# First ternary product of a four-layer kernel: two float32r parts in place of four-pass float32

## The chip, the cores and the metric

The kernel runs on one core of one Trainium2 chip. The metric is the device time of one execution in microseconds. A core has TensorE (PE; its weight loads are listed apart as PEld), VectorE (DVE), ScalarE (ACT), GpSimd (POOL) and SyncE (SP, which here only issues DMAs). Each engine works through its own queue of instructions in order; semaphores hold an instruction back until what it reads or overwrites is ready.

## The reference

Four layers with a residual and a layernorm after each, on x of 8 x 512 x 256 float32:

```python
x = L0_attn_x
x = _layernorm(x + _L0_attn_ref(x, ...))   # retention, 16 heads of 16, group norm
x = _layernorm(x + _L0_ffn_ref(x, ...))    # ternary feed-forward, below
x = _layernorm(x + _L1_attn_ref(x, ...))   # attention across heads within a token
x = _layernorm(x + _L1_ffn_ref(x, ...))    # 8 experts, top 2 of each token, 160 slots
```

The change lies in the second:

```python
def _absmean_core(W):
    gamma = jnp.mean(jnp.abs(W)) + EPS
    Ws = W / gamma
    return jnp.sign(Ws) * jnp.minimum(jnp.round(jnp.abs(Ws)), 1.0), gamma

h = jnp.einsum('btd,hd->bth', x, absmean(W_fc))      # 256 -> 1024: the product that changes
h = jax.nn.gelu(h, approximate=False)
h = layernorm(h, ln_w, ln_b)
return jnp.einsum('bth,dh->btd', h, absmean(W_proj)) # 1024 -> 256
```

The weights of both products are -1, 0 or 1 after `absmean`.

## The kernel before, in words

One batch b is 512 tokens: four chunks of 128 rows, 256 columns. Each batch runs through six stages, written as Python generators:

- a1: transpose x to xT (256 on partitions), products q, k, v (L859, L883), then four chunks of retention: scores `sc` (L907), masked by VectorE, ScalarE and POOL, products into `r_ps` (L927 to L940), the running state (L949).
- a2: group norm, back-transpose (L1038), residual, layernorm. Its result x1 stays in SBUF.
- b: transpose x1 to x1T through `transposed` (L334), which puts four 128x128 transposes into one PSUM bank and copies the bank out with ScalarE, for each of the two halves k of the 256 inputs. Then for each of eight blocks f of 128 hidden units two matmuls of 128x512 into `fc_ps` (L1063), gelu on ScalarE into hT, a square on ScalarE, and a sum of the squares on POOL. Then four products `pr_ps` (L1092, eight matmuls of 128x257 each), with the statistics of the inner layernorm folded into the last step.
- bn: layernorm, plus the scale of the next RMS norm.
- c1: transpose to x2T, project four chunks (L1172, L1178), elu, VectorE transposes, head scores `hs` (L1231), masks, values `at_ps` (L1246).
- c2: a long normalizing part on VectorE, transpose to aT, two products with a gelu between (L1314, L1325), layernorm, transpose to xoT, router product (L1348).

Before them come p(0) (`prepare_ffn`: thresholds, ternary weights, their transposes into fcT and prT, bias sums) and p(1) (`prepare_l1`: the weights of c1 and c2). After the layers each of two groups of four batches is routed, its rows gathered, and 16 expert products run (L1455, L1484), with `finish` writing the output.

The order of instructions is not written by hand. `interleave` keeps the streams in a list, each with its stages in order; it always resumes the stage that can go on first by the plan's clock, and at equal times the one that stands first in the list. A stage says how long its matmuls take with `pe(cost)`, and `op(engine, cost, t, ...)` puts an operation into the first free spell of an engine from time t on. These costs are numbers in the code. They set the order in which each engine's queue is filled; the chip then runs the queues.

Buffers are rings with tags. A stage begins only when its `takes` are free. Tag "T" has three buffers (`TB = 3`, L150) of 128 x 2 x 512 float32 and holds xT (a1), x1T (b), x2T (c1), aT and xoT (c2, through `hold`). PSUM has eight banks of 128x512 float32, also handed out by the plan. The list of streams at L1557 runs: expert weights, x, c2, bn, c1, gather, dispatch, routing, a2, a1, p, b, combine, expert out, expert in, finish. So b ranks last among the stages of the layers.

The lines that matter for the change: `fcT` at L611, its copies at L675, stage b from L1052 to L1076, and the streams of a1, p and b at L1588 to L1599.

Of the kernel before, what the change touches and what calls it, by code (L numbers as in the profile page):

```python
# [10 lines left out]

F32 = mybir.dt.float32
I32 = mybir.dt.int32
AF = mybir.ActivationFunctionType
ALU = mybir.AluOpType
# [4 lines left out]
P = 128  # L20
# [60 lines left out]
def tile_layers(ctx: ExitStack, tc: tile.TileContext, ins, out, at):  # L81
# [82 lines left out]
    def give(tag, t, n=1):  # L164
        Plan.free[tag] += [t] * n
# [8 lines left out]
    def op(engine, cost, t, fn, *args, use=None, drop=None, bank=None, **kw):  # L174


        if engine in (GELU, EXP):
            cost += 0.0 if engine == Plan.loaded else TABLE
            engine, Plan.loaded = ACT, engine
        users = [engine]  # L180
        if engine in (DVS, POOL):
            users.append("port")
        engine = users[0] = {DVS: DVE, POOLD: POOL}.get(engine, engine)
        t = t + HOP
        if use is not None:
            t = max(t, take(use) + HOP)
        if engine != SP:
            length = max(cost - OVERLAP[engine], 0.05)
            found = False
            while not found:  # L190
                found = True
                for user in users:
                    for a, b in Plan.busy[user]:
                        if t + length <= a:
                            break
                        if b > t:
                            t, found = b, False
            for user in users:
                bisect.insort(Plan.busy[user], (t, t + length))
                while Plan.busy[user][0][1] < Plan.t - 30.0:  # L200
                    Plan.busy[user].pop(0)
        Plan.count += 1
        heapq.heappush(Plan.events, (t, Plan.count, lambda: fn(*args, **kw)))  # L203
        t += cost
        if drop is not None:
            give(drop, t)
        if bank is not None:
            release(bank, t)
        return t
# [5 lines left out]
    def pe(cost):  # L215

        Plan.now = Plan.t = max(Plan.now, Plan.t) + cost
        return Plan.now + PE_OUT

    def bank(name):  # L220
        i = Plan.banks.index(min(Plan.banks))
        assert Plan.banks[i] < HELD, name
        ps = psum.tile([P, 512], F32, tag=f"bank{i}", bufs=1, name=name)
        Plan.bank_of[id(ps)] = ps, i
        Plan.banks[i] = HELD
        return ps
# [4 lines left out]
    def need(t, n=1):  # L231

        while True:
            r = max(t + HOP_PE, sorted(Plan.banks)[n - 1] + HOP if n else 0.0)
            yield "pe", r if r < HELD else Plan.t + 0.5
            if not n or sorted(Plan.banks)[n - 1] <= Plan.t + 1e-6:
                return
# [90 lines left out]
    def transposed(dst, src, t, cost=0.5):  # L328

        for k in range(NK):  # L330
            yield from need(t)
            ps = bank("tp")
            for c in range(NC):
                T.transpose(ps[:, c * P : (c + 1) * P], src[:, c, k * P : (k + 1) * P], ident)  # L334
            done = op(ACT, 0.59, pe(cost), A.copy, dst[:, k, :], ps, bank=ps)
        return done
# [214 lines left out]
    with ExitStack() as stages:  # L551
# [56 lines left out]
        op(DVS, 1.0, 15.5, prepare_past)  # L608
        op(DVS, 0.85, 40.0, prepare_gn)

        fcT = fb.tile([P, NK, FF], F32, name="fcT")  # L611


        prT = fb.tile([P, NF, D + 1], F32, name="prT")
# [436 lines left out]

        def stage_b(b):  # L1052
            x1 = x1s.pop(b)
            x1T = wk.tile([P, NK, S], F32, tag="T", bufs=TB, name=f"x1T_{b}")
            turned = yield from transposed(x1T, x1, 0.0)

            hT = fb.tile([P, NF, S], F32, tag="big", bufs=1, name=f"fT_{b}")
            sq = fb.tile([P, S], F32, tag="fsq", bufs=1, name=f"fsq_{b}")
            for f in range(NF):
                yield from need(turned)  # L1060
                ps = bank("fc_ps")
                for k in range(NK):
                    T.matmul(  # L1063
                        ps, fcT[:, k, f * P : (f + 1) * P], x1T[:, k, :],
                        start=(k == 0), stop=(k == NK - 1),
                    )
                inner_ = op(GELU, 0.6, pe(1.73), A.activation, hT[:, f, :], ps, AF.Gelu, bank=ps)
                if f == 0:
                    squared = op(ACT, 0.62, inner_, A.activation, sq, hT[:, f, :], AF.Square)
                else:  # L1070
                    sf = wk.tile([P, S], F32, tag="ex", bufs=EX, name=f"fsf_{b}_{f}")
                    e = op(ACT, 0.63, inner_, A.activation, sf, hT[:, f, :], AF.Square, use="ex")
                    squared = op(
                        POOL, 1.29, max(e, squared), GP.tensor_tensor, sq, sq, sf, ALU.add, drop="ex"
                    )
            give("T", Plan.now)  # L1076
            x1b = x1
            based = op(
                POOL, 2.36, Plan.now, GP.tensor_tensor, x1b, x1, bc(prbias, 1, NC), ALU.add
            )  # L1080
            st = wk.tile([P, 3, NC], F32, tag="f_st", bufs=2, name=f"f_st_{b}")
            z = x1b
            ss = wk.tile([P, NC], F32, tag="f_ss", bufs=2, name=f"f_ss_{b}")
            accs, ends = [], []
            for c in range(NC):
                if c == 1:
                    yield from need(squared, n=2)
                else:
                    yield from need(inner_ - 0.5)
                acc = bank("pr_ps")  # L1090
                for f in range(NF):
                    T.matmul(  # L1092
                        acc[:, : D + 1], hT[:, f, c * P : (c + 1) * P], prT[:, f, :],
                        start=(f == 0), stop=(f == NF - 1),
                    )
                accs.append(acc)
                if c == 1:
                    ps = bank("ss_ps")
                    for i in range(NC):
                        T.matmul(  # L1100
                            ps[:, i : i + 1], sq[:, i * P : (i + 1) * P], ones[:, :1],
                            start=True, stop=True,
                        )
                t = op(
                    DVE, 0.15, pe(4.29 if c == 1 else 3.58), V.tensor_copy,
                    st[:, 0, c : c + 1], acc[:, D : D + 1],
                )
                if c % 2 == 0:
                    continue
                if c == 1:  # L1110
                    op(
                        DVE, 0.16, t, V.tensor_scalar, ss, ps[:, :NC], 1.0 / FF, LN_EPS, ALU.mult,
                        ALU.add, bank=ps,
                    )
                pair = slice(c - 1, c + 1)
                mu, var, rs = (st[:, i, pair] for i in range(3))

                def spread(pair=pair, mu=mu, var=var, rs=rs):

                    nc.vector.tensor_tensor(rs, mu, mu, ALU.mult)  # L1120
                    nc.vector.tensor_tensor(var, ss[:, pair], rs, ALU.subtract)
                    nc.vector.tensor_scalar(var, var, LN_EPS, None, ALU.max)

                t = op(DVS, 0.5, t, spread)
                t = op(
                    POOL, 0.7, t, GP.tensor_tensor, rs, var, mhalf.to_broadcast([P, 2]), ALU.pow
                )
                for c2 in (c - 1, c):
                    ends.append(op(
                        DVE, 0.48, max(t, based), V.scalar_tensor_tensor,  # L1130
                        z[:, c2, :], accs[c2][:, :D], st[:, 2, c2 : c2 + 1], x1b[:, c2, :],
                        ALU.mult, ALU.add, bank=accs[c2],
                    ))
            zs[b] = z, ends
            yield later(Plan.t)
            return Plan.t
# [415 lines left out]
        def after(*keys):  # L1552
            return [k for k in keys if k[1] >= 0 and (k[0] != "p" or k[1] < 2)]
# [32 lines left out]
            [(("a2", b), after(("a1", b)), {}, stage_a2(b)) for b in range(B)]  # L1586
            + [(("o", 0), [], {}, open_experts(0))],
            [  # L1588
                (("a1", b), after(("x", b), ("b", b - 3), ("p", b - 1)), {"aq": 3, "T": 1}, stage_a1(b))
                for b in range(B)  # L1590
            ],
            [
                (("p", 0), [], {"b8": 2}, prepare_ffn()),
                (("p", 1), [], {"m4": 1}, prepare_l1()),
            ],
            [
                (("b", b), after(("a2", b), ("p", 0), ("c1", b - 2)), {"T": 1}, stage_b(b))
                for b in range(B)
            ]  # L1599
            + [(("o", 1), [], {}, open_experts(1))],  # L1600
# [50 lines left out]
```

## Time and profile before

| what | us |
|---|---|
| median of 3 runs (lowest, highest) | 969.6 (968.71, 969.89) |
| the profiled execution, device time | 969.52 |
| its span, first to last instruction | 967.7 |
| TensorE busy | 905.1 |
| VectorE busy | 593.3 |
| ScalarE busy | 459.4 |
| POOL busy | 391.4 |

The span begins with the loading of x and the weights. p(0) ends near 53 us, b(0)'s first block begins at 70 us, and b(7)'s last `pr_ps` ends near 730 us. The experts follow, with the last stages of the layers in between, and `finish` ends the run. The mean granted clock of TensorE was 0.976 of full speed.

In the page, a row of part 5 gives the line, engine, operation, output and inputs, shapes and count, then the group's busy time in us, the mean time of one record in ns, and the idle time of the engine before the group with what ended most of it. L203 is the line in `op` through which all operations of the vector engines go, so for these the tile's name tells the place. Matmul records overlap, so the mean time of a record is longer than its share of the engine. A timeline row gives start, length, engine, line, operation, tiles, count, and in brackets the idle time before it with its releaser. The chain of waits, listed in order of time, gives start, length, engine, tile, line and count.

### The profile page before, as it was taken

How to read it: one execution, taken by the hardware profiler on the slowest of the kernel's cores; microseconds unless marked ns; L12 is line 12 of the kernel's file. 1: busy time of each engine (PE TensorE's matmuls, PEld its weight loads, DVE VectorE, ACT ScalarE, POOL GpSimd, SP SyncE). 2: the span in 40 equal slices, each digit the busy share in tenths (PEclk: the TensorE clock that was granted, in tenths of full speed). 3: DMA queues.
4: the chain of work that ended last, by engine and by line, in shares of the span. 5: the costliest groups of instructions: out<-in, count | busy, mean ns of one | idle time of the engine just before them, and what ended most of it. 6: DMA issues, size and time to landing. Idle time of an engine off the chain costs nothing.

```text
span 967.7 us, 18426 instructions
## 1 busy us (share of the span) xinstructions
PE 905.1 (94%) x7516; PEld 670.7 (69%) x7516; DVE 593.3 (61%) x1469; ACT 459.4 (47%) x868; POOL 391.4 (40%) x395
## 2 busy tenths in 40 slices
PE   7889999999999998999999999999999999999970
PEld 4766766676667665766776567667567798999960
DVE  2943447676766678457767878667756773513223
ACT  2345357347533755178515552763854544222213
POOL 3335434543452345344343453353554233254331
PEclk9999999999999999999999999999999999999985
DMA  7020000001001000100001000105203445429835
GB/s 226 10 88 2 1 1 2 1 23 44 2 1 66 1 2 1 66 2 2 1 22 45 1 2 1 45 2 180 66 1 105 140 146 173 110 53 344 272 64 179
DMA packets 49652, 60.34 MB, mean 62 GB/s; under 512 B 5536, under 2 KB 44960, under 8 KB 49568
## 3 DMA queue, kind: packets, MB, share of 16 engines
q1 hardware_dynamic: 45600, 53.92, 16.4%
q0 software_dynamic: 3968, 5.25, 3.0%
q8 instruction: 59, 0.97, 0.4%
q14 instruction: 25, 0.20, 0.1%
HBM read 43.43 MB, written 15.73 MB: 61 GB/s over the span
## 4 chain that ended last, share of the span: by engine, by line
PE 73%; DVE 15%; ACT 4%; POOL 3%; issue 3%; DMA 2%; POOLq 0%; ACTq 0%; SPq 0%; DVEq 0%; another core or an unknown queue 0%
PE fc_ps L1063 10%; PE pr_ps L1092 7%; PE wo_ps L1484 7%; PE wi_ps L1455 6%; PE qk_ps L1172 5%; PE qk_ps L859 5%; PE hs L1231 3%; PE at_ps L1246 3%; PE tp L334 3%; PE w_ps L1314 3%; DVE a L203 2%; PE r_ps L940 2%; PE v_ps L1178 2%; PE w_ps L1325 2%; PE sc L907 2%
## 5 line engine op out<-in xcount | busy, mean ns | idle before, releaser
L1092 PE MATMUL pr_ps<-prT,fT 128*128 128x257 f32 x512 | 118.4, 385 | 3.0 <-ACT aT L203 2.8
L1063 PE MATMUL fc_ps<-x1T,fcT 128*128 128x512 f32 x256 | 118.7, 601 | 1.4 <-ACT x1T L203 1.4
L1092 PEld LDWEIGHTS pr_ps<-prT,fT 128*128 128x128 f32 x512 | 96.1, 191 | 19.2 <-ACT aT L203 3.0
L203 POOL TENSOR_TENSOR fsq<-fsq,fsf 128x512 f32<-128x512 f32 x56 | 71.8, 1281 | 65.4 <-ACT fsf L203 65.0
L1063 PEld LDWEIGHTS fc_ps<-x1T,fcT 128*128 128x128 f32 x256 | 45.7, 190 | 47.7 <-issue 40.7
L1455 PE MATMUL wi_ps<-xsT,wi 128*128 128x160 f32 x512 | 74.9, 301 | 0.0
L1484 PE MATMUL wo_ps<-e_hT,wo 128*128 128x160 f32 x512 | 74.3, 300 | 0.0
L1484 PEld LDWEIGHTS wo_ps<-e_hT,wo 128*128 128x128 f32 x512 | 70.9, 190 | 1.5 <-issue 1.3
L1455 PEld LDWEIGHTS wi_ps<-xsT,wi 128*128 128x128 f32 x512 | 70.6, 190 | 0.7 <-ACT xsT L203 0.4
L203 DVE TENSOR_TENSOR hm<-hs,cst 128x512 f32<-128x512 f32 x96 | 59.8, 675 | 16.8 <-PE hs L1231 15.7
L203 POOL DMA_INDIRECT y_d<-eo,srci x24 | 37.5, 1560 | 80.3 <-ACT eo L203 26.5
L203 DVE TENSOR_TENSOR scm<-sc,cst 128x512 f32<-128x512 f32 x96 | 60.4, 679 | 14.3 <-PE sc L907 14.2
L203 POOL TENSOR_TENSOR ln_rs<-ln_rs,mhalf 128x4 f32<-128x4 f32 x32 | 34.3, 1073 | 81.1 <-DVE ln_rs L203 79.5
L203 ACT ACTIVATE e_hT<-wi_ps 128x480 f32<-128x480 f32 (+1 forms) x48 | 24.9, 526 | 86.6 <-PE wi_ps L1455 86.6
L203 POOL TENSOR_TENSOR scm<-scm,cst 128x512 f32<-128x512 f32 x32 | 41.6, 1300 | 50.3 <-ACT scm L203 50.3
L1172 PE MATMUL qk_ps<-l1T,x2T 128*128 128x512 f32 x128 | 61.4, 602 | 0.0
L859 PE MATMUL qk_ps<-xT,wqkv 128*128 128x512 f32 x128 | 60.2, 610 | 0.1
L203 DVE STREAM_TRANSPOSE hT<-pad 128x512 f32<-128x512 f32 x64 | 59.3, 960 | 0.5 <-POOL pad L203 0.5
L203 POOL TENSOR_SCALAR pad<-pad,lamv 128x128 f32<-128x128 f32 x32 | 12.0, 375 | 111.2 <-DVE pad L203 111.2
L203 ACT ACTIVATE fT<-fc_ps 128x512 f32<-128x512 f32 x64 | 38.2, 597 | 34.9 <-PE fc_ps L1063 34.7
L203 ACT ACT_TABLE_LOAD x39 | 50.0, 1283 | 1.4 <-PEq L1637 0.7
L203 POOL TENSOR_TENSOR hm<-hm,cst 128x512 f32<-128x512 f32 x32 | 41.1, 1284 | 22.0 <-ACT hm L203 22.0
(233 smaller groups left out, 1850.4 us busy)
## 6 DMA issues: line engine op xcount, KB each, us to landing
wi<-in_L_ffn_wi SPq DMA_DIRECT2D x13, 1024.0 KB, 6.8
wo<-in_L_ffn_wo SPq DMA_DIRECT2D x13, 1024.0 KB, 9.1
x<-in_L_attn_x SPq DMA_DIRECT2D x8, 512.0 KB, 3.7
x_d<-a SPq DMA_DIRECT2D x8, 512.0 KB, 2.8
y_d<-a SPq DMA_DIRECT2D x8, 512.0 KB, 3.7
z<-y_d SPq DMA_DIRECT2D x8, 512.0 KB, 7.1
out<-z SPq DMA_DIRECT2D x8, 512.0 KB, 2.8
prepare<-in_L_ffn_W_fc SPq DMA_DIRECT2D x1, 1024.0 KB
```

The source lines that it names most:

```text
L203: heapq.heappush(Plan.events, (t, Plan.count, lambda: fn(*args, **kw)))
L334: T.transpose(ps[:, c * P : (c + 1) * P], src[:, c, k * P : (k + 1) * P], ident)
L859: T.matmul(ps, wqkv[:, k, which * D + m * P : which * D + (m + 1) * P], xT[:, k, :], start=(k == 0), stop=(k == NK - 1),)
L907: T.matmul(sc[p][:, m * 256 : (m + 1) * 256], kT[rows, m, cs], qz[c][rows, m, :, :], start=True, stop=True,)
L1063: T.matmul(ps, fcT[:, k, f * P : (f + 1) * P], x1T[:, k, :], start=(k == 0), stop=(k == NK - 1),)
L1092: T.matmul(acc[:, : D + 1], hT[:, f, c * P : (c + 1) * P], prT[:, f, :], start=(f == 0), stop=(f == NF - 1),)
L1172: T.matmul(qk, x2T[:, k, cs], l1T[:, k, 0:2, :].rearrange("p a d -> p (a d)"), start=(k == 0), stop=(k == NK - 1),)
L1231: T.matmul(sc[r][:, g * P : (g + 1) * P], hT[rows, g, P : 2 * P], hT[rows, g, :P], start=True, stop=True,)
L1246: T.matmul(acc[32 * r : 32 * r + 32, g * P : (g + 1) * P], vt[:, g, 32 * r : 32 * r + 32], scm[r][:, g, :], start=True, stop=True,)
L1314: T.matmul(ps, l1T[:, k, 3, m * P : (m + 1) * P], aT[:, k, :], start=(k == 0), stop=(k == NK - 1),)
L1455: T.matmul(ps[:, f * CAP : (f + 1) * CAP], wi[:, k, (f3 + f) * P : (f3 + f + 1) * P], x[:, k, es], start=(k == 0), stop=(k == NK - 1),)
L1484: T.matmul(ps[:, m * CAP : (m + 1) * CAP], wo[:, f, m * P : (m + 1) * P], hT[:, f, :], start=(f == 0), stop=(f == NF - 1),)
```

## The change

- fcT becomes float32r; its four ScalarE copies write this type.
- Stage b no longer calls `transposed`. It transposes the same way, but ScalarE copies the PSUM bank into a float32r tile `high`, and VectorE subtracts `high` from the bank into a second float32r tile `low`. The bank is released after the subtraction.
- For each block f the two float32 matmuls become four float32r ones, low and high for each half k, all into the same bank. The planner's cost of a block goes from 1.73 to 0.95.
- Stage b takes and gives back two buffers of tag "T" in place of one; the ring still has three.
- In the list of streams, p stands ahead of a1 in place of behind it.

```diff
+F32R = mybir.dt.float32r
...
-        fcT = fb.tile([P, NK, FF], F32, name="fcT")
+        fcT = fb.tile([P, NK, FF], F32R, name="fcT")
...
-            x1T = wk.tile([P, NK, S], F32, tag="T", bufs=TB, name=f"x1T_{b}")
-            turned = yield from transposed(x1T, x1, 0.0)
+            high, low = (
+                wk.tile([P, NK, S], F32R, tag="T", bufs=TB, name=f"x1T_{b}_{i}") for i in "hl"
+            )
+            for k in range(NK):
+                yield from need(0.0)
+                ps = bank("tp")
+                for c in range(NC):
+                    T.transpose(ps[:, c * P : (c + 1) * P], x1[:, c, k * P : (k + 1) * P], ident)
+                t = op(ACT, 0.59, pe(0.5), A.copy, high[:, k, :], ps)
+                turned = op(
+                    DVE, 0.68, t, V.tensor_tensor, low[:, k, :], ps, high[:, k, :], ALU.subtract,
+                    bank=ps,
+                )
...
                 for k in range(NK):
-                    T.matmul(
-                        ps, fcT[:, k, f * P : (f + 1) * P], x1T[:, k, :],
-                        start=(k == 0), stop=(k == NK - 1),
-                    )
-                inner_ = op(GELU, 0.6, pe(1.73), A.activation, hT[:, f, :], ps, AF.Gelu, bank=ps)
+                    for x in (low, high):
+                        T.matmul(
+                            ps, fcT[:, k, f * P : (f + 1) * P], x[:, k, :],
+                            start=(k == 0 and x is low), stop=(k == NK - 1 and x is high),
+                        )
+                inner_ = op(GELU, 0.6, pe(0.95), A.activation, hT[:, f, :], ps, AF.Gelu, bank=ps)
...
-            give("T", Plan.now)
+            give("T", Plan.now, 2)
...
             [
+                (("p", 0), [], {"b8": 2}, prepare_ffn()),
+                (("p", 1), [], {"m4": 1}, prepare_l1()),
+            ],
+            [
                 (("a1", b), after(("x", b), ("b", b - 3), ("p", b - 1)), {"aq": 3, "T": 1}, stage_a1(b))
                 for b in range(B)
             ],
             [
-                (("p", 0), [], {"b8": 2}, prepare_ffn()),
-                (("p", 1), [], {"m4": 1}, prepare_l1()),
-            ],
-            [
-                (("b", b), after(("a2", b), ("p", 0), ("c1", b - 2)), {"T": 1}, stage_b(b))
+                (("b", b), after(("a2", b), ("p", 0), ("c1", b - 2)), {"T": 2}, stage_b(b))
```

## The prediction, made before the changed kernel was run

> **What bounds the kernel now.** I read the page's busy table and slices first, to see which engine has no slack and where.
>
> ```profile
> span 967.7 us, 18426 instructions
> PE 905.1 (94%) x7516; PEld 670.7 (69%) x7516; DVE 593.3 (61%) x1469; ACT 459.4 (47%) x868; POOL 391.4 (40%) x395
> PE   7889999999999998999999999999999999999970
> DVE  2943447676766678457767878667756773513223
> PEclk9999999999999999999999999999999999999985
> ```
>
> TensorE has a nine in almost every slice up to the last, while VectorE swings between four and eight. The last 26 us have no matmul. Busy time of a pipelined engine can flatter, so I read the chain of waits next, then the groups:
>
> ```profile
> PE 73%; DVE 15%; ACT 4%; POOL 3%; issue 3%; DMA 2%; POOLq 0%; ACTq 0%; SPq 0%; DVEq 0%; another core or an unknown queue 0%
> PE fc_ps L1063 10%; PE pr_ps L1092 7%; PE wo_ps L1484 7%; PE wi_ps L1455 6%; PE qk_ps L1172 5%; PE qk_ps L859 5%; PE hs L1231 3%; PE at_ps L1246 3%; PE tp L334 3%; PE w_ps L1314 3%; DVE a L203 2%; PE r_ps L940 2%; PE v_ps L1178 2%; PE w_ps L1325 2%; PE sc L907 2%
> ```
>
> ```profile
> L1092 PE MATMUL pr_ps<-prT,fT 128*128 128x257 f32 x512 | 118.4, 385 | 3.0 <-ACT aT L203 2.8
> L1063 PE MATMUL fc_ps<-x1T,fcT 128*128 128x512 f32 x256 | 118.7, 601 | 1.4 <-ACT x1T L203 1.4
> L1063 PEld LDWEIGHTS fc_ps<-x1T,fcT 128*128 128x128 f32 x256 | 45.7, 190 | 47.7 <-issue 40.7
> ```
>
> The line to be changed, L1063, is the largest on the chain. Its 128 program matmuls (8 batches x 8 blocks x 2) are 256 records: two records each. The 601 ns of one is no cost, since records overlap. The cost is the start-to-start step, which the chain in order of time gives:
>
> ```profile
> 706.75 7.06 PE fc_ps L1063 x16
> 716.52 7.15 PE pr_ps L1092 x32
> 725.47 3.69 PE pr_ps L1092 x16
> ```
>
> Sixteen L1063 records follow each other in 7.06 us including the first's start; in the many pieces of x4 the same view has 1.72 us, so one block f (4 records) costs **1.72 us**. For pr_ps, pieces of x16 elsewhere in that view take 3.48 us: 0.2175 us per record of 257 columns.
>
> **What the Trainium skill says.** "FP8 and Floating Point Precision", TensorE Precision Notes: true fp32 is four passes; a reduced form reads the 4-byte value and truncates it, with no pass count or time. The trace agrees with four: if a record is two passes, pr_ps streams 2 x 257 columns in 217.5 ns, 0.423 ns a column, and L1063 2 x 512 in 0.43 us, 0.420 ns. "TensorE: Matmul & The Clock Gate", "Wait — 56ns, not 53.3ns?", gives N / 2.4 + 2.5 ns for a back-to-back pass; 512 columns make 215.8 ns, in line with that. The same page, Part 1, says that an idle array falls to half clock. The trace fits: the mean clock was 0.98, 0.98 and 0.97 in 250-340, 340-430 and 430-520 us, the stretches with waits, and 1.00 in 72-160.
>
> **The change, part by part.** Everything is counted against the profiled execution: 969.5 us, of which the span is 967.7; the median of the runs is 969.6, the same.
>
> *Matmuls.* Each block has four one-pass records instead of four two-pass ones. No float32r record exists in this trace. Price by the pr_ps row: 512 x 0.423 = 0.217 us, a block 0.867. Low bound 0.863 (the page's price), high bound the 0.95 that the diff gives its planner; the old 1.73 there is the trace's 1.72. Weight loads stay four a block; one takes 190 ns, and pr_ps already runs loads of 191 ns at a 217 ns step (wi_ps at 136 ns), so they stay hidden. Gain (1.72 - 0.867) x 64 = **54.6 us** (49.3 to 54.8). All of it lies on the saturated engine.
>
> *Splitting the rows.* The 16 ScalarE copies PSUM to x1T (601 ns) stay, now with rounded output; I take no extra. New: 16 VectorE subtractions of a PSUM and an SBUF operand, 128x512. The nearest row:
>
> ```profile
> L203 DVE TENSOR_TENSOR x<-r_tp,x 128x512 f32<-128x512 f32 x16 | 10.3, 680 | 7.4 <-PE r_tp L1038 7.4
> ```
>
> 16 x 0.68 = 10.9 us on VectorE, busy 447.5 of the 658 us between 72 and 730. It would be 458 of about 615, 75%: no new bound on average. But the first matmul now waits for copy and subtraction, 0.73 us later per batch with the hop. Matmuls wait for x1T already (1.4 us), so cover is thin: 0 to 8 x 0.73 = 5.8; I take 3. The transposes' PSUM banks are also held 0.7 us longer; with eight banks I take nothing, inside the same bound. Behind the waiting subtraction on VectorE stand c1's and a1's mask products (679 ns each), which matmuls wait for; that delay is part of the cover item below. An added dependency cannot gain.
>
> *The ring T.* Stage b takes two of three buffers. Seen here:
>
> ```profile
> 416.75 3.70 PE L1063 MATMUL fc_ps<-x1T,fcT 128*128 128x512 f32 x8
> 422.83 1.04 PE L334 MATMUL tp<-cst_ident,x 128*128 128x128 f32 x8
> 442.56 1.07 PE L334 MATMUL tp<-cst_ident,x 128*128 128x128 f32 x8
> 449.81 1.03 PE L1178 MATMUL v_ps<-l1T,x2T 128*128 128x256 f32 x4
> 470.30 3.60 PE L1063 MATMUL fc_ps<-x1T,fcT 128*128 128x512 f32 x8
> ```
>
> b runs from before 416.75 to 473.7; c1's x2T (the transposes at 422.83) lives to 450; a1's xT starts at 442.56. That is 2 + 1 + 1 = 4 of 3 for 7 us, and again at 514-522 us, where the three stages start together. In most other batches they don't overlap. a1 or b then starts later, but a1's output is needed only some 60 us afterwards, and b itself ends sooner. 0 to 2 x 7 = 14 us; I take 3.
>
> *Cover used up.* This is the largest unknown. The layer phase, 72 to 730 us, has only 15.6 us of TensorE idle (658 - 642.4), since b, the stage of lowest rank, fills gaps. c2 normalizes on VectorE for some 20 us at a time, and matmuls wait at its end:
>
> ```profile
> 385.96 5.12 PE L1092 MATMUL pr_ps<-prT,fT 128*128 128x257 f32 x16 [2.78 <-ACT aT L203]
> 490.83 1.66 PE L334 MATMUL tp<-cst_ident,a 128*128 128x128 f32 x8 [2.06 <-DVE a L203]
> ```
>
> In these tails (263-283, 368-386, 466-492) two blocks of L1063, 3.6 us, stand as cover. Halving them exposes 1.7 us in each of six tails, 10 us; if b ends earlier its followers can start earlier too, and nothing is exposed. I take 5 (0 to 15, as VectorE's queue fills). Two more half-clock spells after such waits: 2 us (0 to 5). The new matmuls ride the chip at the same clock.
>
> *Stage p before a1 in the list.* The list's place decides ties alone. The planner gives TensorE to p's transposes and to its 3.5 us sums pr_bias and pr_mean first; a1(0)'s chunks, queued behind, wait, and p ends sooner, which a1(1) and b(0) wait for. Its DMAs (two weight loads and two vectors on SP's queue) are issued when p starts, at 4.3 to 5.7 us, as before; those of p(1) (the l1 weights, on SP) and its two memsets on POOL follow p(0)'s end and move with it, ahead of nothing that waits at that time. -2 to +2; I take 0. Experts (after 730) and the tail are only shifted.
>
> *Sum.* -54.6 + 3 + 3 + 5 + 2 = -41.6; 969.5 - 41.6 = 927.9, say **928 us**.
>
> **Rivals.**
> - *Full gain.* List scheduling keeps TensorE filled whatever stage b weighs: the 15.6 us of idle stay, only x1T's 3 us are lost. 969.5 - 54.6 + 3 = 918. For it: VectorE is at 75%, ScalarE lower; against: the waits at c2's tails.
> - *Cover gone.* The chain of c1 and c2 (215-306 us in the third round, 91 us against an 88 us round) sets the pace, and half of each batch's gain turns to waiting: 969.5 - 27 + 3 = 945. For it: VectorE is at 73.7 of 90 us in 520-610; against: the next c1 waits for b's pr_ps, which comes sooner.
> - *float32r takes two cycles a column*, at L1063. Then a record costs 0.43 us as now, a block 1.72, and nothing pays for the subtraction and the ring: 969.5 + 3 + 3 = 976, slower. It decides from a record of about 0.40 us on, where 64 x 4 x (0.43 - 0.40) = 7.7 us no longer covers those losses. Here the change would not do what it says. For it: all fp32 streams here move a new column every 0.84 ns (two passes), so nothing shows a 4-byte operand read faster; a transpose of 128 columns also steps at 109 ns. Against: a transpose also needs a weight load each time, which may be what sets its step.
>
> **How the numbers follow.** Forecast 928 (0.60, own range 920 to 940); full gain 918 (0.14); cover gone 945 (0.19); two cycles 976 (0.07). Low end: 969.5 - 54.8 with no loss and p's 2 us, 913, rounded to 914. High end: 969.5 - 49.3 + 5.8 + 14 + half of cover's upper ends (10) = 950, cut to 949 since these do not come together. What is left out is the 0.07 and a few in a hundred on each side. Within 0.2% (about 2 us, what a measurement of this kernel can tell from no change) almost nothing lies: 0.02. Faster 0.91, slower 0.07.
>
> **What would show it.** Right: L1063 pieces of x4 in 0.87 us instead of 1.72; TensorE busy down by some 50 us to about 855; 16 new subtractions of about 0.68 us; the last matmul near 895 instead of 937; idle TensorE in the layer phase 20 to 30 us. Wrong: records 0.4 us apart (two cycles); idle over 40 us with waits for a, x2T or scm (cover gone); transposes of x held until a last v_ps or fc_ps (ring).

## The result, and the profile after

The changed kernel takes **979.1 us** (median of 8 runs, 975.7 to 983.7). The kernel before took 969.7 us beside it (8 runs, 968.7 to 972.1). The ratio is 1.0097, with a 95% interval of 1.0068 to 1.0126. The forecast was 928 with a range of 914 to 949; the kernel became about 1% slower.

The profiled execution of the changed kernel took 982.84 us, in the upper part of its runs; its span is 981.1. These are the lines of its page that answer to those of before: busy time by engine, then the slices.

```profile
span 981.1 us, 18435 instructions
PE 879.1 (90%) x7516; PEld 687.0 (70%) x7516; DVE 602.1 (61%) x1485; ACT 453.2 (46%) x866; POOL 393.8 (40%) x395
PE   7799999998969899999999989968979999999870
DVE  2954466579656768686786788676865743502213
PEclk9999999998879999999999989998989999999985
```

TensorE is busy for 26.0 us less (905.1 to 879.1), but the span is 13.4 us longer. Eights, sixes and sevens now stand in the row of TensorE's slices, and eights and a seven in the row of its clock, where there were nines. VectorE has 16 more instructions and 8.8 us more busy time. The page's chain of waits can't be compared with that of before: in this trace it breaks off after the last few per cent ("PE 2%; DMA 1%; ..."), so I read the groups, the waits and the timeline.

The groups of the changed matmuls and of the new subtraction, and c2's product `t`, which is needed below:

```profile
L1079 PE MATMUL fc_ps<-x1T_l,fcT 128*128 128x512 f32 x128 | 53.9, 421 | 0.3 <-ACT scm L204 0.3
L1079 PE MATMUL fc_ps<-x1T_h,fcT 128*128 128x512 f32 x128 | 50.3, 393 | 0.0
L204 DVE TENSOR_TENSOR x1T_l<-tp,x1T_h 128x512 fp32r<-128x512 f32 x16 | 10.6, 677 | 3.2 <-ACT x1T_h L204 3.2
L204 DVE SCALAR_TENSOR_TENSOR t<-g3b,rms_ss,a 128x256 f32<-128x256 f32 x32 | 22.6, 758 | 4.6 <-POOL rms_ss L204 4.5
```

Again the length of a matmul record is no cost; the step is. Four records of one block, from the timeline:

```profile
77.33 0.48 PE L1079 MATMUL fc_ps<-x1T_l,fcT 128*128 128x512 f32 x1
77.65 0.39 PE L1079 MATMUL fc_ps<-x1T_h,fcT 128*128 128x512 f32 x1
77.88 0.40 PE L1079 MATMUL fc_ps<-x1T_l,fcT 128*128 128x512 f32 x1
78.11 0.39 PE L1079 MATMUL fc_ps<-x1T_h,fcT 128*128 128x512 f32 x1
```

The second starts 0.32 us after the first, the others 0.23 us apart. Over the whole trace the median step is 0.231 us, so the steps of a block make 0.92 us where they made 1.72. The change did what it says: 64 x (1.72 - 0.92) = 51 us of work are gone. Counted over all records instead, each from its start to the start of the next, without waits and half clock, `fc_ps` takes 63.9 us where it took 113.5: 50 us less. What has come in their place is waiting. Of TensorE's waits, the ones in the layers that grew most, and the only one of the changed matmuls, with the total in us, the number of times and the longest:

```profile
PE tp L335 <- DVE a L204: 21.8, 4, 8.5
PE tp L335 <- ACT x L204: 15.4, 9, 10.2
PE hs L1247 <- DVE scm L204: 4.0, 1, 4.0
PE fc_ps L1079 <- ACT scm L204: 0.3, 1, 0.3
```

Before, the first two of these were 7.2 us (longest 2.1) and 1.5 us (longest 1.0), and the third didn't exist. The last line is all that the changed matmuls themselves wait: 0.3 us, and for no part of the split. Beyond the layers, the transposes `eo_tp` of the experts wait 6.6 us where they waited 1.2. The four longest waits on the timeline (start, length, engine, line, what; in brackets the idle time before it):

```profile
241.41 3.26 PE L1247 MATMUL hs<-hT 16*128 16x128 f32 x30 [4.04 <-DVE scm L204]
278.62 1.97 PE L335 MATMUL tp<-cst_ident,a 128*128 128x128 f32 x8 [8.46 <-DVE a L204]
664.91 2.80 PE L335 MATMUL tp<-cst_ident,x 128*128 128x128 f32 x8 [10.22 <-ACT x L204]
732.49 1.97 PE L335 MATMUL tp<-cst_ident,a 128*128 128x128 f32 x8 [7.00 <-DVE a L204]
```

Eight transposes that take 1.04 us elsewhere take 1.97 and 2.80 us after these waits. They start 0.213 us apart where 0.109 was read before: half clock. (The first four of x start 0.49 us apart, since ScalarE delivers them chunk by chunk.) For the layer phase, 72 to 730 us, the row of the stages begins (length, TensorE busy, then the other engines) with 658 us and 609.05:

```profile
72.00:730.00 658.00, 609.05 (x5452) 453.66 (x5451) 461.61 (x1114) 351.74 (x658) 288.05 (x291) 0.96 0.06 21
```

So 49 us of it are idle where 15.6 were, and the clock is 0.96 where it was 0.99.

To put all kernels on one scale I split the time up to the last matmul into work at full clock (busy time less half of the busy time in which the clock was half), the loss to half clock (that half), and idle time. The three add up to the end of the last matmul. Each row is one profiled execution, not the median of the runs:

```
kernel                         last matmul = full work + half clock + idle   (us)
before                           937.0         896.9        8.2      31.9
after                            950.1         850.6       28.5      71.0
```

So 46.3 us less work, 20.3 us more half clock and 39.1 us more idle time: +13.1 us.

### The profile page after: what moved, and what is told of

Its sections match the earlier page's. It is cut to its first block, busy times and chain, and to the rows that moved or that the text cites. A ratio compares the mean times of both kernels' runs of the same rounds, so it can differ in the third digit from the quotient of the medians.

```text
span 981.1 us, 18435 instructions
## 1 busy us (share of the span) xinstructions
PE 879.1 (90%) x7516; PEld 687.0 (70%) x7516; DVE 602.1 (61%) x1485; ACT 453.2 (46%) x866; POOL 393.8 (40%) x395
## 5 line engine op out<-in xcount | busy, mean ns | idle before, releaser
L1108 PE MATMUL pr_ps<-prT,fT 128*128 128x257 f32 x512 | 122.0, 392 | 1.2 <-DVE scm L204 0.7
L1108 PEld LDWEIGHTS pr_ps<-prT,fT 128*128 128x128 f32 x512 | 98.6, 196 | 17.8 <-DVE scm L204 1.1
L1471 PE MATMUL wi_ps<-xsT,wi 128*128 128x160 f32 x512 | 78.6, 308 | 0.0
L1471 PEld LDWEIGHTS wi_ps<-xsT,wi 128*128 128x128 f32 x512 | 74.1, 197 | 0.6 <-issue 0.2
L1079 PE MATMUL fc_ps<-x1T_l,fcT 128*128 128x512 f32 x128 | 53.9, 421 | 0.3 <-ACT scm L204 0.3
L1079 PE MATMUL fc_ps<-x1T_h,fcT 128*128 128x512 f32 x128 | 50.3, 393 | 0.0
L1247 PE MATMUL hs<-hT 16*128 16x128 f32 x1024 | 40.6, 289 | 4.0 <-DVE scm L204 4.0
```

The costliest lines, as they stand in the source:

```text
L1079: T.matmul(ps, fcT[:, k, f * P : (f + 1) * P], x[:, k, :], start=(k == 0 and x is low), stop=(k == NK - 1 and x is high),)
L1108: T.matmul(acc[:, : D + 1], hT[:, f, c * P : (c + 1) * P], prT[:, f, :], start=(f == 0), stop=(f == NF - 1),)
L1247: T.matmul(sc[r][:, g * P : (g + 1) * P], hT[rows, g, P : 2 * P], hT[rows, g, :P], start=True, stop=True,)
L1471: T.matmul(ps[:, f * CAP : (f + 1) * CAP], wi[:, k, (f3 + f) * P : (f3 + f + 1) * P], x[:, k, es], start=(k == 0), stop=(k == NK - 1),)
```

## The experiments

Two theories are to be told apart. **Order**: the planner gets a new cost (0.95), a new number of buffers, a new operation and a new list, so it fills every engine's queue in another order, and that order has long waits. **Arithmetic**: the new dependency, the added VectorE work and the shorter cover of the matmuls make the waits, whatever the order. The expectations of e1 to e4 were written before the first theory was: their "chain" and "subtraction" are the arithmetic (freed time turns into waits; VectorE's added work costs the gain), their "ring" and "list" are the second buffer and p's place. In the kernels below that keep an order, the operations of TensorE, VectorE, ScalarE and POOL stand in their traces in the same sequence as in the kernel named, apart from those that the text names.

**The order of before, with one-pass matmuls** (e1). The planner still sees 1.73, so its order stays. The low part and its subtraction are left out; the high part is multiplied twice.

```diff
-            x1T = wk.tile([P, NK, S], F32, tag="T", bufs=TB, name=f"x1T_{b}")
+            x1T = wk.tile([P, NK, S], F32R, tag="T", bufs=TB, name=f"x1T_{b}")
...
-                    T.matmul(
-                        ps, fcT[:, k, f * P : (f + 1) * P], x1T[:, k, :],
-                        start=(k == 0), stop=(k == NK - 1),
-                    )
+                    for i in range(2):
+                        T.matmul(
+                            ps, fcT[:, k, f * P : (f + 1) * P], x1T[:, k, :],
+                            start=(k == 0 and i == 0), stop=(k == NK - 1 and i == 1),
+                        )
```

> The kernel before, its order of instructions untouched (planner's cost 1.73, one buffer of T, p behind a1): only fcT and x1T are float32r, and each float32 matmul of L1063 becomes two one-pass ones on the same rounded x1T. The low part and its subtraction are left out, so a block has the four records of the change. Theory chain (the layers' chains through VectorE and ScalarE set the pace, and TensorE's freed time turns into waits and half-clock spells): 950 to 968 us, TensorE idle before its last matmul up from 32 to some 60 us or more. Theory ring/list (the two buffers of T or p's place cost what the matmuls gain): 920 to 930. Theory subtraction (the added VectorE work costs it): 920 to 930 as well.

Measured: 946.6 us (946.5 to 948.3), ratio 0.976 (0.973 to 0.978). That is in none of the ranges, below that of "chain" and above those of the others. The one-pass matmuls alone gain 23 us. TensorE waits for a 8.9 us in all, the longest 3.6, not 21.8 and 8.5.

**The same with the planner's cost of the change** (e2).

```diff
-                inner_ = op(GELU, 0.6, pe(1.73), A.activation, hT[:, f, :], ps, AF.Gelu, bank=ps)
+                inner_ = op(GELU, 0.6, pe(0.95), A.activation, hT[:, f, :], ps, AF.Gelu, bank=ps)
```

> As e1_order_kept, but the planner is told 0.95 a block, so that the order is planned anew; still one buffer of T, no low part, no subtraction, p behind a1. Theory chain: the new order doesn't help, 955 to 985 us, idle TensorE 60 to 75 us. Theories ring/list and subtraction: 915 to 930.

Measured: 983.9 us (982.1 to 987.0), ratio 1.014 (1.011 to 1.017). One number of the planner, with the same work on the chip, takes 37 us. Idle time goes from 41.3 (e1) to 70.2 us. Time and idle lie in the ranges of "chain", but "chain" has no reason for a difference from e1.

**The kernel before with p ahead of a1** (e3), and **with two buffers for b in the plan** (e4). Neither changes any work.

```diff
-            give("T", Plan.now)
+            give("T", Plan.now, 2)
...
-                (("b", b), after(("a2", b), ("p", 0), ("c1", b - 2)), {"T": 1}, stage_b(b))
+                (("b", b), after(("a2", b), ("p", 0), ("c1", b - 2)), {"T": 2}, stage_b(b))
```

> The kernel before with p ahead of a1 in the list of streams, nothing else. Theory chain: within 5 us of before (965 to 975). Theory list: 980 or more.

> The kernel before with stage b taking and giving two buffers of T in the plan (the second unused), nothing else. Theory chain: within 8 us of before (962 to 978). Theory ring: 990 or more, with x1's transposes held back by a c2 or c1.

Measured: 981.9 us (ratio 1.011, 1.009 to 1.013) and 981.9 us (1.011, 1.009 to 1.013). Both cost 12 us. For e3 that is the range of "list" (980 or more), for e4 it lies between its two. In e4 the second buffer is counted but not used, so the chip waits for nothing more than before; only the plan changed. The two are no sum either, since the kernel with both of them, the new cost and the subtraction stands at 979.

**The whole arithmetic in the order of before** (e5): high, low and subtraction, 16 subtractions put in without being planned. To make room, low has a buffer of its own, `vt` and `kd` have one buffer fewer, and `g2` is read in place of its wide copy.

```diff
-            x1T = wk.tile([P, NK, S], F32, tag="T", bufs=TB, name=f"x1T_{b}")
-            turned = yield from transposed(x1T, x1, 0.0)
+            high = wk.tile([P, NK, S], F32R, tag="T", bufs=TB, name=f"x1T_{b}")
+            low = fb.tile([P, NK, S], F32R, tag="low", bufs=1, name=f"low_{b}")
+            turned = yield from transposed(high, x1, 0.0, low=low)
```

> The whole arithmetic of the change (high and low, the subtraction, one-pass matmuls) in the order of the kernel before: the planner sees the old costs, the low part has a buffer of its own, and the 16 subtractions are slipped into VectorE's queue behind their copies without being planned. Room for it comes from one buffer less of vt and of kd and from g2 used as it is in place of its copy g2b. Theory order (the newly planned order, not the added work, costs the change its gain): 945 to 956 us, little over e1_order_kept's 946.6. Theory subtraction: 965 or more.

Measured: 955.1 us (951.4 to 960.1), ratio 0.984 (0.982 to 0.986). This is in the range of "order". It computes what the changed kernel computes, 24 us faster, and beats both. It also stands 27 us above the forecast of 928 and outside its range. Its profile is of its slowest run (960.1).

**The changed kernel with the old cost in its plan** (e6: 0.95 back to 1.73, nothing else).

> The changed kernel, but the planner is told the old 1.73 a block; two buffers of T and p ahead as in the change. Theory order: another order, so another time, not settled by this cost alone; 955 to 985. If the price of 0.95 alone were to blame: 945 to 952.

Measured: 992.1 us (986.4 to 993.1), ratio 1.0215 (1.018 to 1.025): above what I expected. The new cost isn't the culprit by itself; with the old one the plan is yet another, and a slower one.

**The order of the changed kernel with the matmuls of before** (e7): float32, two matmuls a block on the copy; low is computed and not used.

```diff
-                    for x in (low, high):
-                        T.matmul(
-                            ps, fcT[:, k, f * P : (f + 1) * P], x[:, k, :],
-                            start=(k == 0 and x is low), stop=(k == NK - 1 and x is high),
-                        )
+                    T.matmul(
+                        ps, fcT[:, k, f * P : (f + 1) * P], high[:, k, :],
+                        start=(k == 0), stop=(k == NK - 1),
+                    )
```

> The changed kernel's order of instructions with the old matmuls: fcT and both x1T tiles in float32, two four-pass matmuls a block on the copy, the low part computed and not used. Theory order: the order carries its loss with it, so slower than the kernel before by about what the change lost against e1: 990 to 1020 us. Theory chain alone (time set by chains whatever the matmuls cost): about the changed kernel's 979.

Measured: 1022.4 us (1020.5 to 1023.7), ratio 1.055 (1.053 to 1.057), a little over the expectation. In this order the new matmuls are worth 43 us (both kernels do the subtractions); in the old one 23 (e1, where neither does). Its waits:

```profile
PE tp L335 <- DVE a L204: 17.7, 4, 7.5
PE tp L335 <- ACT x L204: 16.1, 13, 10.2
PE hs L1246 <- DVE scm L204: 4.0, 1, 4.0
```

**The order of the changed kernel without the low part** (e11): the subtractions are planned but not issued, and the high part is multiplied twice.

> The changed kernel with its order of all instructions kept, but the low part and its 16 subtractions left out: the high part is multiplied twice, so the product is not that of the reference. In the order of before the same omission was worth 8.5 us. Theory that the newly planned order itself carries the loss: 968 to 978 us, still above the 946.6 of the same work in the order of before. Rival, that the subtraction in the planned order (VectorE's time and the wait for it) carries the loss: below 960 us.

Measured: 977.0 us (974.1 to 980.6, 20 runs), ratio 1.006 (1.004 to 1.0075). Leaving the split out gives back 2 us of the changed kernel's time (4 by the two ratios). Its timeline at the same places:

```profile
278.40 1.97 PE L335 MATMUL tp<-cst_ident,a 128*128 128x128 f32 x8 [8.46 <-DVE a L204]
664.09 2.80 PE L335 MATMUL tp<-cst_ident,x 128*128 128x128 f32 x8 [10.22 <-ACT x L204]
729.78 1.97 PE L335 MATMUL tp<-cst_ident,a 128*128 128x128 f32 x8 [7.00 <-DVE a L204]
```

These are the waits of the changed kernel to the hundredth of a us. Side by side, all waits of over 1.8 us between 60 and 900 us, in order:

```
after   2.00  2.40  4.04  8.46  2.20  3.95  2.23  10.22  7.00  2.13
e11     2.00  2.41  4.04  8.46  2.21  3.96  2.23  10.22  7.00
e7      2.00  2.40  4.04  7.51  2.21  3.15  2.22  10.22  4.67
```

With the split or without it, with matmuls of 0.92 or of 1.72 us a block, the same instructions of TensorE wait for the same tiles for about the same time. The order carries them. Nor is it the cover: in e7 the blocks are as long as before the change, and the waits still come; the short blocks add 0.8 to 2.3 us to three of them. All three kernels also share the second tile of T. It isn't what holds them: in the changed kernel's trace, wherever ScalarE stood idle ahead of a copy into a tile of T, it waited for the transposes and never for a matmul that still read the buffer.

**The changed kernel with dummies** (e8): 38 matmuls of 128x512 of no use, 0.86 us each, ahead of seven groups of transposes that wait, to keep the array awake.

```diff
             ps = bank("tp")
+            for _ in range(warm if k == 0 else 0):
+                T.matmul(ps, ident, cst[:, :512], start=True, stop=True)
```

> The changed kernel with 38 dummy matmuls of 128x512 on constants (0.86 us each at full clock) ahead of those transposes of a and x that TensorE stood waiting for in the changed kernel's trace, into the bank that the transposes then overwrite: they run in time that was idle, so that the clock need not fall. Half clock during work was 57 us and cost some 28 us there. Theory clock: mean clock from 0.948 to about 0.965 and 965 to 973 us. If the half-clock spells cost nothing of the end: 977 to 983.

Measured: 968.7 us (966.9 to 970.4, 12 runs), ratio 0.999 (0.998 to 1.000). Work of no use takes off 10 us. The mean clock goes from 0.948 to 0.969, and the loss to half clock from 28.5 to 14.4 us. So the half clock after the waits costs some 10 us of the changed kernel's time, and isn't only their companion.

**The e5 kernel with 15 dummies** (e9), and **with the two high parts of a block first** (e10).

```diff
-                for k in range(NK):
-                    for x in (low, high):
+                for x in (high, low):
+                    for k in range(NK):
```

> The change's whole arithmetic in the order of the kernel before (955.1 us), with 15 added 128x512 matmuls of no use, 0.86 us each, put on TensorE just ahead of its waits for the low part (batches 1, 2, 4, 6) and for c2's a (batches 2, 3, 5, 6). They fill time in which the array would stand idle. Theory that part of what the kept order loses is the half clock after short waits (24.4 us lost to it in that kernel, counted as half of the 48.7 us of half-clock work): 943 to 950 us. Rival, that the half clock is only a companion of the waits: 954 to 960.

> The change's whole arithmetic in the order of the kernel before (955.1 us), but each block of the first product takes the two high parts first and the two low parts after them, so that the subtraction has 0.46 us longer. Theory that the waits for the low part (8.3 us in six places, up to 2.4 us) cost what separates 955.1 from the 946.6 without a low part: six times 0.46 us shorter waits and perhaps one or two half-clock spells fewer, 949 to 953 us. Rival, that the low part costs by VectorE's time and not by the wait ahead of it: no change, 954 to 957.

Measured: 953.2 us (949.5 to 958.9), ratio 0.981 (0.974 to 0.988), and 955.3 us (949.8 to 956.7), ratio 0.982 (0.975 to 0.988). Both beat both kernels, but neither can be told from e5, whose four runs spread over 9 us. So neither theory is settled: e9 falls between its two ranges, e10 into that of its rival. The waits that they aimed at did shrink. For low, in e5 and then in e10:

```profile
PE fc_ps L1071 <- DVE low L342: 8.3, 6, 2.4
```

```profile
PE fc_ps L1071 <- DVE low L342: 2.8, 6, 0.7
```

So the wait for low isn't shown to be what separates e5 (955.1) from e1 (946.6).

## Why the prediction was wrong

All kernels on the scale from above. The profiled execution is not the median: it took 982.8 us of the changed kernel, and in e5 and e6 it is the slowest of four.

```
kernel                              median us   last matmul = full work + half clock + idle
before: old order, four passes         969.7      937.0         896.9        8.2      31.9
e1: old order, one pass, no low        946.6      913.9         856.6       16.0      41.3
e5: old order, the whole change        955.1      927.5         854.2       24.4      48.9
e9: e5 with dummies                    953.2      921.1         868.9       16.3      36.0
e10: e5 with high first                955.3      921.7         859.8       16.2      45.7
e7: new order, four passes            1022.4      988.5         900.0       23.8      64.7
e11: new order, one pass, no low       977.0      943.5         850.6       24.9      68.0
after: new order, the whole change     979.1      950.1         850.6       28.5      71.0
e8: after with dummies                 968.7      937.5         885.0       14.4      38.0
e3: before, p ahead                    981.9      949.7         900.0       14.6      35.1
e4: before, two buffers in the plan    981.9      950.0         900.2       10.6      39.2
e2: e1 with the planner's 0.95         983.9      950.2         853.5       26.5      70.2
e6: after with the planner's 1.73      992.1      960.2         860.6       22.2      77.4
```

The same change of order, at three kinds of work: 1022.4 - 969.7 = +53 us with four passes, 977.0 - 946.6 = +30 with one pass and no low, 979.1 - 955.1 = +24 with the whole change. Of the middle pair, which does the same work in both orders, 26.7 us is idle time, 8.9 us half clock, and -6.0 us work. Only the middle pair is like for like: e7 also does the subtractions that the kernel before lacks, and e5 has fewer buffers for `vt` and `kd`. In both orders the one-pass matmuls gain. What turns the gain into a loss is the order.

The order is not the whole miss. Of the 51 us between the forecast and the result, it accounts for 24 (e5's 955 to 979). The other 27 (928 to 955) are there with the order kept. In e5's profile work falls by 42.7 us, not 54.6, and idle time and half clock grow by 17.0 and 16.2, where the sum had 13 for all losses together.

**The steps that failed** are two. The first stands in no line of the sum, and that is the fault: a new plan was put at nothing. "Full gain" says that list scheduling keeps TensorE filled whatever b weighs, "Stage p before a1" prices p's place as a matter of ties, and the sum starts from an idle time of 15.6 us "in the layer phase" as if it belonged to the kernel. It belongs to one order. The four inputs that the diff changes for the planner (cost, buffers, list, operation) make a different schedule each, and all of those that I ran are slower than the first at the same work: e3 and e4 by 12 us, e2 by 37, e7 by 53.

The second is "All of it lies on the saturated engine", with 5 us for cover and 2 for half clock against it. In e1, with the order kept and neither split nor second buffer, 23 us arrive: work falls by 40, and 17 turn into idle time (9.4) and half clock (7.8).

Point by point:

- *Matmuls*: right in mechanism, a little off in size. The steps of a block took 0.92 us, not 0.867, inside the bounds: 51 us, not 54.6. "Cover gone", with 945, is nearer to e1 than the forecast is. Its reason, a chain of c1 and c2 that sets the pace, was not tested alone: e1's waits for a grow only from 7.2 to 8.9 us. In the same order (e7 to the changed kernel) work falls by 49.4 us. Against the kernel before it falls by 40 in e1, although `fc_ps` itself, counted from start to start, loses 48: `hs` and `at_ps` take 7 us more. Why they do is open.
- *Two cycles a column*: refuted by the step of 0.231 us.
- *Splitting the rows*: 16 x 0.677 = 10.8 us on VectorE, as priced. The matmuls waited for no part of it in the changed kernel (3 taken) and 8.3 us in e5 (upper bound 5.8), where nobody had planned the subtraction. The cost in time is 2 to 4 us in the new order (e11) and 8.5 in the old one (e5 against e1).
- *The ring T*: taken as 3 us of waiting (0 to 14). e4, which only counts the second buffer, costs 12 through the plan: 7.3 us of idle time, 2.4 of half clock and 3.3 of work. The size is within the range, the way is another. The sign that was named for the ring, transposes held by another stage's last matmul, does not show in the changed kernel.
- *Stage p before a1*: taken as 0 (-2 to +2). Alone it costs 12 us (e3): the largest miss against its own bounds. "Ties alone" plays the list down: `interleave` lifts the time of every stage that could already go on to the plan's clock, so stages tie whenever several are ready, and the list is their rank. "Experts and the tail are only shifted" missed the waits of `eo_tp`, 6.6 us after 1.2 (1.2 in e5 too, 4.1 in e11).
- *Cover used up*: 5 us (0 to 15) was the right kind of loss and far too small: 39 us more idle time. Most of that was not the cover: in e7 idle time is up by 33 us with blocks as long as before, in e1 by 9.4 with short ones. "Two more half-clock spells" became eleven after four between 60 and 900 us, four of them 10.2 us long, and the loss grew by 20.3 us. By e8 about 10 of these are won back when the waits are filled.
- One reading was off without consequence: the end of the kernel before without a matmul is 30.7 us long (937.0 to 967.7), not 26.

How such a wait comes about can be read from the one that ends at 278.62 us. In TensorE's queue the transposes of a come right after sixteen records of `pr_ps`, with nothing of another stage between, while c2 still normalizes on VectorE. The end of VectorE's part of that chain:

```profile
271.62 1.48 DVE L204 SCALAR_TENSOR_TENSOR t<-g3b,rms_ss,a 128x256 f32<-128x256 f32 x1
273.10 4.21 DVE L204 SCALAR_TENSOR_TENSOR t<-g3b,rms_ss,a 128x256 f32<-128x256 f32 x3
277.34 1.23 DVE L204 TENSOR_TENSOR a<-a,t 128x1024 f32<-128x1024 f32 x1
```

and POOL's timeline beside it:

```profile
271.56 1.26 POOL L204 TENSOR_TENSOR scm<-scm,cst 128x512 f32<-128x512 f32 x1
272.78 4.25 POOL L204 TENSOR_TENSOR fsq<-fsq,fsf 128x512 f32<-128x512 f32 x3
```

Four products `t` take 5.7 us; the median of all 32 is 0.48 us, so four take 1.9 undisturbed. They go in step with POOL's additions, which belong to stage b. The Trainium skill, "SBUF — State Buffer", section "Who interferes with whom", says that a VectorE instruction with two SBUF inputs contends with a POOL instruction that reads SBUF, since the second input comes through ports that the two share under an exclusive lock. The trace agrees: 1.40 us per `t` beside 1.32 to 1.44 us per addition, so that each `t` waits for about one addition. These 3.8 us are nearly half of this wait of 8.46; no run takes them out alone. The planner does know of the port: `op` books `t` and all of POOL's operations in one list, "port", so that they don't overlap in the plan. On the chip they met. Over the trace the mean of `t` rose from 660 to 758 ns, 32 x 0.098 = 3.1 us, so this explains a part of one wait and not the loss.

The wait that ends at 664.91 is another thing. TensorE's next instructions are the transposes of the x that stage bn normalizes. On VectorE b's output for it is there at 656.4, but its statistics stand behind c2's normalization:

```profile
655.59 0.87 DVE L204 SCALAR_TENSOR_TENSOR x<-pr_ps,f_st,x 128x256 f32<-128x256 f32 x2 [0.23 <-POOL f_st L204]
659.17 1.23 DVE L204 TENSOR_TENSOR a<-ap,hs 128x1024 f32<-128x1024 f32 x1
660.43 1.22 DVE L204 TENSOR_TENSOR a<-a,g2b 128x1024 f32<-128x1024 f32 x1
661.57 0.42 DVE L347 BATCH_NORM_STATS2 ln_st<-x 128x6 f32<-128x256 f32 x1
```

They begin at 661.57, 5.1 us after b's output is done: half of the 10.22 us is VectorE's own order.

**What stays open.** The runs show that the order makes the 24 us between e5 and the changed kernel, not why the planner's rule makes a worse one from these inputs. Each of five changed plans came out worse, which speaks for the order of before as an unusually good one, but five are too few to say how the rest spread. What the 8.5 us between e5 and e1 are made of is open too: shortening the wait for low from 8.3 to 2.8 us moved the median by nothing that can be told.

## What to carry to other kernels

Where a planner fills the queues from costs, an edit of a cost, a buffer count or a rank is an edit of the whole schedule. Price it by making such an edit alone, with no change of work (here 12 us, twice), and keep that spread in the range of any forecast. To learn what an operation is worth, hold the order fixed and change only the operation; then decide on the order by itself: here the kept order made a change that lost 1% into one that gains 1.6% (e5). And work taken from an engine that is busy nine tenths of the time isn't all time won: the same 51 us gave 23 us in one order (e1) and 43 in another (e7 to the changed kernel).

## What the runs showed of the hardware that was not expected

- A float32r matmul of 128x512 steps at 0.231 us, against 0.429 for each of the two records of a float32 one. That is 7% more than the 0.2158 us that the Trainium skill gives a pass ("TensorE: Matmul & The Clock Gate", "Wait — 56ns, not 53.3ns?"), though its weight loads, 188 ns each, still fit under it.
- Waits of 2 us can be followed by half clock. Up to the last matmul the spells in the traces last 3.4, 6.8, 10.2 or 13.7 us, and in the changed kernel those that begin at 130.76, 202.44 and 274.12 us lie 21 times 3.41 us apart. The Trainium skill, same page, Part 1, has half clock follow at least one idle window of about 3.4 us. The window's length agrees; the need for a whole idle one doesn't, since a spell of 3.4 us begins at 130.8 after a wait of 2.00 us. Nor is 2 us a threshold: the wait of 2.20 us ahead of 329.3 has no spell. Of the waits of 8.46 and 7.00 us, spells of 10.2 us begin within the wait, at 274.1 and 728.1. What runs in a spell takes about twice as long (0.213 us a transpose, not 0.109), on top of the wait.
- The 38 dummies of e8 put 32.7 us of matmuls of no use into the queue and made the kernel 10 us faster.
